# A fused two-layer block on one core: loads moved behind key stores, first key norms on VectorE, wider steps, and four key tasks moved into the attention units

## The chip, the cores and the metric

The kernel runs on one NeuronCore of a Trainium2 chip. The metric is the device time of one execution in microseconds (us); of several executions the median is taken. TensorE (PE) multiplies matrices, VectorE (DVE), ScalarE (ACT) and GpSimd (POOL) work on elements, and SyncE (SP) and POOL issue DMAs. Each engine runs its own instructions strictly in order and waits on semaphores of the others.

## What is computed

x has the shape (4, 512, 512): 4 batches of 512 rows, handled as 16 tiles of 128 rows. Four residual blocks follow each other:

```
x = x + ssm(ctx, layernorm(x))            # state-space scan over ctx
x = x + experts(layernorm(x))             # 64 experts, 8 per row, weighted sum
q = rmsnorm(layernorm(x) @ Wq, gq)        # 16 heads of 128
k = rmsnorm(ctx @ Wk, gk); v = ctx @ Wv
x = x + softmax(q @ k.T / sqrt(128)) @ v @ Wo
x = x + ffn(layernorm(x))                 # weights and activations quantized
```

Everything but the quantized parts is float32.

## The kernel before

The program has three stages: the state-space stage, the expert stage and the attention stage with the feed-forward work. The change lies at the seam of the last two and inside the third.

**Key tasks.** The keys of a batch b and head h are one *key task* (class `Keys`): `task` multiplies Wk of the head with ctx of the batch on PE (two matmuls of 128x512, shown by the profile as four passes, L1231), `evict` squares the result on ACT (L1241), scales it into SBUF as kT (L1243) and stores kT to k_dram through SP (L1246), `squares` sums the squares with four matmuls against ones (L1255), and `take` writes the mean squares with ACT (L1267). The 64 key tasks are placed wherever PE is thought to have room. Nine are done in the expert stage, one after each of the first experts (`key_tasks`, called from `run_in`): heads 6 and 7 of batches 2 and 3, and heads 3 to 7 of batch 1. Sixteen are left for the attention stage (`KEYS_LATE`: heads 8 to 15 of batches 2 and 3): eight among its first steps, eight in its units. The inverse roots of their mean squares are made for all late keys at once in `last_keys`, and stored as rows in r_dram.

**First steps of attention** (`attend`, 1436 to 1530 us of the profile). PE can't start a head before the four row tiles of batch 0 have their expert outputs. For each tile, POOL issues eight gathers from y_dram (`fetch`, L1876; a gather moves 128 rows of 2 KB, 256 KB), DVE adds each to x with its weight (`add`, L1884), and then come the layernorm statistics (`stats`: two DVE operations and two of POOL, ve and rstd), the normalized tile (`normed`, DVE, xn_c), its transpose on PE (`turn_x`, copied by ACT), and for each of two head groups the queries: `queries` (PE pq, ACT squares), `norm_q` (DVE sum, POOL qms and rq), `scale_q` (DVE qn) and `turn_q` (PE pqt, ACT qT). `scores` then starts the first head: PE psc, DVE maximum mx, ACT exponential e; `weights` and `turn` divide and transpose e. Between these stand eight key tasks (`some_keys`) and the loads `load_q` (Wq of a head group, 1 MB) and `load_kv` (kT, its norm row rk broadcast to 128 partitions, and v: 256 KB each). `norm_k` multiplies kT by rk, on POOL (L1944).

The order of all this is written out by `later(time, f)`: a list of steps with nominal times, sorted, and then emitted in that order. So a nominal time fixes only the order in which each engine gets its instructions, not when they run. GAP = 1.25 is the distance of two gathers; FLIGHT = 3.5 the distance of a gather and its add. The gathers of the four tiles follow each other without a break, so the last additions of a tile stand among the first of the next one. Gathers use four buffers in turn; `wide` gives tile 0 four more.

**Units.** From then on the order is by units: unit u = 4n+i handles row tile i of head n; `put(front/back, u, ...)` hangs other work onto units, the eight remaining key tasks among it (units 7, 11, ... 35; sums one unit later), and `last_keys`.

Buffers in the pool `late` are shared by tag: "Th" and "hq" hold the ctx of batches and later feed-forward tiles, "hid" holds Wk of eight heads.

Of the kernel before, what the change touches and what calls it, by code (L numbers as in the profile page):

```python
# [29 lines left out]
P = 128  # L30
# [27 lines left out]
HG = 4  # L58

KEYS_LATE = [(b, h) for b in (2, 3) for h in range(8, H)]  # L60
# [730 lines left out]
def moe_phase(ctx, cm, x_all, w, kv, dr, router_stats, out):  # L791
# [28 lines left out]
    with tc.manual_schedule():  # L820
        attend(cm, x_all, w, kv, y_dram, r["wk"], r["pos"], tern, late, ctx_k, keys.wk, out)
# [380 lines left out]
class Keys:  # L1202
# [14 lines left out]
    def load(self, h0, h1, pool, tag):  # L1217

        t = pool.tile([P, self.KC, (h1 - h0) * HD], F32, name="k_w", tag=tag)
        for h in range(h0, h1, HG):  # L1220
            cols = slice(h * HD, min(h + HG, h1) * HD)
            self.nc.sync.dma_start(t[:, :, cols.start - h0 * HD:cols.stop - h0 * HD],
                                   self.w["Wk"][:, cols].rearrange("(k p) e -> p k e", p=P))
        for h in range(h0, h1):
            self.wk[h] = t[:, :, (h - h0) * HD:(h - h0 + 1) * HD]
# [9 lines left out]
    def evict(self, vec=None):  # L1235

        if self.pk is None:
            return
        b, h, pk = self.pk
        sq, kT = self.row("sq"), self.row("kT")  # L1240
        self.nc.scalar.activation(sq, pk, AF.Square)  # L1241
        if vec is None:
            self.nc.scalar.activation(kT, pk, AF.Copy, scale=self.cm.gkq)  # L1243
        else:
            vec.tensor_scalar(kT, pk, self.cm.gkq, None, ALU.mult)
        self.nc.sync.dma_start(self.kv["k"][b, h], kT)  # L1246
        self.pk, self.sq = None, (b * H + h, sq)
# [11 lines left out]
    def take(self):  # L1259
        if self.pss is None:  # L1260
            return
        i, pss = self.pss
        if self.direct is None:
            ms = self.small.tile([P, self.KB], F32, name="k_ms")
        else:
            ms, self.direct = self.direct[:, 0:self.KB], self.direct[:, self.KB:]
        self.nc.scalar.activation(ms, pss, AF.Copy, bias=EPS, scale=1.0 / HD)  # L1267
        if self.direct is None:
            self.nc.sync.dma_start(self.kv["ms"][:, i * self.KB:(i + 1) * self.KB], ms)
        self.pss = None  # L1270
# [178 lines left out]
def key_tasks(keys, w, pool, late, ps):  # L1449

    nc = keys.nc
    left = [(b, h) for b in (2, 3) for h in (6, 7)] + [(1, h) for h in range(3, H // 2)]
    late_b = KEYS_LATE[0][0]
# [5 lines left out]
    def load(b0, h0, b, h):  # L1459

        if b != b0:
            t = ctx[b] = late.tile([P, CTX // P, S], F32, name="k_ctx",
                                   tag="hq" if b > late_b else "Th")
            nc.sync.dma_start(t, w["ctxT"][:, b * S:(b + 1) * S].rearrange("(k p) s -> p k s",
                                                                           p=P))
        if h // (2 * HG) != h0 // (2 * HG):
            h0 = h // (2 * HG) * 2 * HG
            keys.load(h0, h0 + 2 * HG, late, "hid")

    def task(n):  # L1470
        keys.task(*left[n])
        keys.evict()
        if n + 1 < len(left):
            load(*left[n], *left[n + 1])
        else:
            load(*left[n], late_b, KEYS_LATE[0][1])

    load(-1, -1, *left[0])
# [366 lines left out]
def attend(ctx, cm, x_all, w, kv, y_dram, wk, pos, tern, late, ctx_k, wk_k, out):  # L1845
# [95 lines left out]
    def norm_k(n):  # L1941
        if n < len(heads):
            kT, rk = ks[n]
            nc.gpsimd.tensor_tensor(kT, kT, rk, ALU.mult)  # L1944
# [252 lines left out]
    ms = pool[1].tile([P, n_ms], F32, name="k_ms")  # L2197
    inside = [False]

    def key_row(n):  # L2200

        if not inside[0]:
            return pool[7].tile([P, S], F32, name=f"k_{n}", tag="oT")
        return (late.tile([P, S], F32, name="k_kT", tag="Th") if n == "kT" else
                pool[1].tile([P, S], F32, name="k_sq", tag="xn_d"))

    def key_bank(shape, name):
        if name == "kpss":
# [5 lines left out]
                lambda b: (ctx_k[b], 0), direct=ms)  # L2214
    keys.wk = wk_k
    first = KEYS_LATE[0][1]
    load_q(0)
    load_kv(0)
# [6 lines left out]
    GAP, FLIGHT = 1.25, 3.5  # L2225

    wide = pool[1].tile([P, KB, S], F32, name="yg_first", tag="eT")
    for n in range(NC * TOPK):
        later(n * GAP, fetch, 1, wide[:, n - KB] if KB <= n < 2 * KB else None)
        later(n * GAP + FLIGHT, add, 1)  # L2230
    for i in range(NC):
        end = (i + 1) * TOPK * GAP + FLIGHT
        later(end, stats, i, "c")
        later(end + 2.5, normed, i, "c")
        later(end + 3, turn_x, i)
        for g, t in ((0, end + 4), (1, end + 9)):
            later(t, queries, 0, g, i)
            later(t + 5.5, norm_q, 0, g)
            later(t + 8, scale_q, 0, g)
            later(t + 8.5, turn_q, 0, g, i)  # L2240
        later(end + 14, scores, 0, i)
        if i < KB - 1:
            later(end + 18, weights, 0, i)
        if i < KB - 2:
            later(end + 19, turn, 0, i)
    for f, n, time in ((load_q, 1, 6), (load_kv, 1, 12), (load_kv, 2, 18),
                       (norm_k, 0, 20.5), (norm_k, 1, 30.5), (norm_k, 2, 40.5)):
        later(time, f, n)

# [6 lines left out]
    def last_keys():  # L2256
        rsqrt(nc, small, ms, ms, "late")
# [10 lines left out]
    for i in range(H // 2):  # L2268
        later(2.6 * i if i < 7 else 22, some_keys, *KEYS_LATE[i])
# [9 lines left out]
    for i in range(H // 2):  # L2279
        u = KB * (i + 1) + 3  # L2280
        put(front, u, keys.task, *KEYS_LATE[H // 2 + i])
# [3 lines left out]
    put(back, KB * (H // 2 + 1) + 4, last_keys)  # L2285
# [141 lines left out]
```

## Time and profile before

| what | value |
|---|---|
| median of 3 runs | 2722.08 us (2715.19 to 2722.46) |
| the profiled execution: its time / its span | 2716.06 us / 2714.3 us |
| mean granted PE clock | 0.96 |
| PE busy | 2519.8 us, 93% of the span |
| DVE, ACT, POOL busy | 1519.0, 1234.1, 1175.4 us |
| attention's first PE work / end of the first steps | 1436.5 us / 1529.5 us |

The span is the profiled execution from first to last instruction. "Busy" is the time in which an engine had an instruction in work; "granted clock" is the share of full speed that PE got. The chain of waits follows the work that ended last backwards to what released each step. In a timeline, the number in brackets is how long the engine sat idle before a line, and who released it.

### The profile page before, as it was taken

Reading aid. Unit: us, or ns where it says so; the run is one execution under the profiler, and the core shown is the slowest. Engines: PE = TensorE matmul, PEld = TensorE weight load, DVE = VectorE, ACT = ScalarE, POOL = GpSimd, SP = SyncE. Lnnn points to the kernel's source line nnn. Section 1 sums busy time; section 2 is a strip of 40 time slices with the busy share of each in tenths; the row PEclk is TensorE's granted clock in tenths of the full one; section 3 lists DMA queues with packets and bytes.
Section 4 is the critical chain, followed back from the end, with each engine's and each line's share of the span. In section 5 each row is a group of like instructions: output and inputs, shape, how many; then the busy total and the mean of one; then the engine's idle time right before and its main releaser. Section 6 shows DMA issues by size and latency. Waiting matters only on the chain. (4 is left out here: it accounts for less than half of the span.)

```text
span 2714.3 us, 29922 instructions
## 1 busy us (share of the span) xinstructions
PE 2519.8 (93%) x10151; PEld 1428.1 (53%) x10151; DVE 1519.0 (56%) x2575; ACT 1234.1 (45%) x2351; POOL 1175.4 (43%) x1073
## 2 busy tenths in 40 slices
PE   5989797887899999999998899999999999999997
PEld 2545454554556566666674454445555555555543
DVE  5897989966322244344324555546665666554446
ACT  5666666664323222233322344344555555555543
POOL 3888888960333344444435323223332343211112
PEclk8979798998999999999998899999999999999999
DMA  6253535332656567889866444223332343222100
GB/s 247 90 196 104 199 103 185 117 133 83 203 177 218 187 220 224 284 276 330 279 224 213 125 135 126 87 95 117 128 101 74 120 128 113 70 82 62 56 31 20
DMA packets 199358, 404.67 MB, mean 149 GB/s; under 512 B 30611, under 2 KB 72147, under 8 KB 195104
## 3 DMA queue, kind: packets, MB, share of 16 engines
q1 hardware_dynamic: 156574, 249.33, 27.6%
q0 software_dynamic: 40576, 153.19, 18.0%
q8 instruction: 83, 1.36, 0.2%
q14 instruction: 75, 0.61, 0.1%
q10 hardware_dynamic: 2050, 0.18, 0.1%
HBM read 320.70 MB, written 81.92 MB: 148 GB/s over the span
## 5 line engine op out<-in xcount | busy, mean ns | idle before, releaser
L1989 DVE TENSOR_REDUCE mx<-psc 128x1 f32<-128x512 f32 x256 | 176.8, 691 | 459.0 <-PE psc L1986 459.0
L1335 PE MATMUL pg<-xT,wg 128*128 128x284 f32 (+12 forms) x1536 | 400.9, 405 | 2.1 <-ACT xT L1322 1.1
L1335 PEld LDWEIGHTS pg<-xT,wg 128*128 128x128 f32 x1536 | 283.6, 195 | 86.3 <-issue 38.3
L521 POOL TENSOR_TENSOR dBu<-bb,du 128x1024 f32<-128x1024 f32 x128 | 318.1, 2508 | 21.5 <-DVE dA L546 13.6
L1992 ACT ACTIVATE e<-psc,mx 128x512 f32<-128x512 f32 x256 | 176.0, 688 | 309.7 <-DVE mx L1989 309.4
L1986 PE MATMUL psc<-kT,qT 128*128 128x512 f32 x512 | 267.1, 604 | 1.0 <-ACT qT L1980 1.0
L1276 POOL DMA_INDIRECT xg<-xn_dram,tok x168 | 172.1, 1024 | 215.1 <-PE pt L1319 169.8
L2013 PE MATMUL po<-eT,v 128*128 128x512 f32 x512 | 231.5, 595 | 8.1 <-ACT eT L2007 8.0
L1952 PE MATMUL pq<-Wq,xnT 128*128 128x512 f32 x512 | 235.8, 604 | 0.7 <-DMA k_dram<-k_kT 0.7
L2022 PE MATMUL px<-Wo,oT 128*128 128x512 f32 x512 | 231.9, 597 | 0.0
L532 ACT ACTIVATE dA<-delta,negA 128x512 f32<-128x512 f32 x256 | 176.8, 694 | 86.9 <-DVE hc L547 76.6
L2006 PEld LDWEIGHTS pet<-ident,e 128*128 128x128 f32 x1024 | 127.8, 142 | 146.2 <-issue 119.8
L1963 POOL TENSOR_SCALAR qms<-qms 128x4 f32<-128x4 f32 x64 | 24.8, 388 | 413.2 <-DVE qms L1961 412.4
L546 DVE TENSOR_TENSOR_SCAN dA<-dA,dBu 128x1024 f32<-128x1024 f32 x80 | 184.9, 2311 | 21.1 <-POOL dBu L521 14.6
L552 PE MATMUL yT<-ident,hc 128*128 128x128 f32 x1024 | 143.4, 290 | 41.1 <-POOL hc L547 23.7
L552 PEld LDWEIGHTS yT<-ident,hc 128*128 128x128 f32 x1024 | 127.1, 151 | 100.7 <-issue 56.3
L1380 DVE COPY yo<-po 128x512 f32<-128x512 f32 x68 | 47.0, 691 | 219.2 <-PE po L1369 219.2
L2013 PEld LDWEIGHTS po<-eT,v 128*128 128x128 f32 x512 | 96.3, 190 | 134.3 <-issue 115.9
L1876 POOL DMA_INDIRECT yg<-y_dram,pos x124 | 125.4, 1011 | 87.0 <-issue 62.9
L2006 PE MATMUL pet<-ident,e 128*128 128x128 f32 x1024 | 155.3, 275 | 7.7 <-DVE e L1998 7.7
L2007 ACT COPY eT<-pet 128x512 f32<-128x512 f32 x256 | 148.0, 578 | 6.1 <-PE pet L2006 6.1
L1276 POOL DMA_INDIRECT wd<-down,widx x64 | 63.4, 990 | 200.9 <-PE po L1369 169.0
(356 smaller groups left out, 4442.2 us busy)
## 6 DMA issues: line engine op xcount, KB each, us to landing
y_dram<-yo SPq DMA_DIRECT2D x110, 256.0 KB
bb<-bc_dram SPq DMA_DIRECT2D x16, 1024.0 KB
cb<-bc_dram SPq DMA_DIRECT2D x16, 1024.0 KB
v_dram<-v SPq DMA_DIRECT2D x64, 256.0 KB
k_dram<-k_kT SPq DMA_DIRECT2D x64, 256.0 KB
Wq<-Wq SPq DMA_DIRECT2D x16, 1024.0 KB
kT<-k_dram SPq DMA_DIRECT2D x64, 256.0 KB
rk<-r_dram SPq DMA_DIRECT2D x64, 256.0 KB
```

The lines of the kernel that those rows point to most:

```text
L521: nc.gpsimd.tensor_tensor(dBus[q], st[b]["bb"][i // 2][:, j:j + 2, :], st[b]["du"][c].unsqueeze(1).to_broadcast([P, 2, S]), ALU.mult)
L532: nc.scalar.activation(dAs[q][:, j, :], st[b]["delta"][c], AF.Exp, scale=negA[:, c, n:n + 1])
L546: nc.vector.tensor_tensor_scan(*flat, 0.0, ALU.mult, ALU.add)
L552: nc.tensor.matmul(yT[:, lc, :], t[:, lc * P:(lc + 1) * P], cm.ident, is_transpose=True, start=first and lc == 0, stop=last, skip_group_ch ...
L1276: nc.gpsimd.indirect_dma_start(out=t[0:n, :], out_offset=None, in_=table, in_offset=bass.IndirectOffsetOnAxis(ap=index, axis=0))
L1335: nc.tensor.matmul(pg[:, 0:n], s["wg"][:, c, m * P:(m + 1) * P], s["xT"][:, c, 0:n], start=c == 0, stop=c == NC - 1)
L1952: nc.tensor.matmul(pq.rearrange("p h d -> p (h d)"), xnTs[b * NC + i][:, c, :], s["Wq"][:, c, :], start=c == 0, stop=c == NC - 1)
L1986: nc.tensor.matmul(pscore, st[b, g]["qT"][:, h, i * P:(i + 1) * P], ks[n], start=True, stop=True)
L1989: nc.vector.tensor_reduce(mx, pscore, AX.X, ALU.max, negate=True)
L2006: nc.tensor.transpose(pt[:, kc, :], e[:, kc * P:(kc + 1) * P], cm.ident)
L2013: nc.tensor.matmul(po, v[:, kc, :], eT[:, kc, :], start=kc == 0, stop=kc == KB - 1)
L2022: nc.tensor.matmul(px, oTs[j * HG + h][:, i * P:(i + 1) * P], st[b, g]["Wo"][:, h, :], start=h == 0, stop=h == HG - 1)
```

## The change

- `KEYS_LATE` begins at head 6: heads 6 and 7 of batches 2 and 3 leave the expert stage (five key tasks are left there, and ctx is loaded three times for them rather than four) and go to the units, which now hold twelve key tasks (units 7 to 51); `last_keys` moves from unit 40 to unit 56. Late keys go in the order of heads, batches 2 and 3 in turn; both ctx stay in "Th" and "hq". Wk of heads 6 and 7 is loaded over that of heads 8 and 9 (`load_last`) during the first steps. In the units kT is made and stored in two halves of 256 columns, in the buffers "xq" and "Tx".
- `load_kv(0)` was issued by SP before anything else but Wq; now it comes at nominal time 8.1, behind the stores of the first four key tasks. The other loads move from 6, 12, 18 to 13.3, 17, 25.
- The first three `norm_k` run on VectorE instead of GpSimd.
- Tiles start 12 apart (TILE) instead of 10, FLIGHT is 5 instead of 3.5, `wide` also serves tile 1, and the steps that follow a tile's last add stand 0.5 to 1.7 nearer to it. In the emitted order, each tile's statistics and `normed` now stand on DVE ahead of the next tile's adds; the first head's maximum of tile i-1 (mx) and the second group's query sum (qms) of tile i-1 now stand on DVE ahead of `normed` of tile i, where they stood behind it; and on PE psc of tile i-1 is ahead of the transpose of tile i.

```diff
-KEYS_LATE = [(b, h) for b in (2, 3) for h in range(8, H)]
+KEYS_LATE = [(b, h) for b in (2, 3) for h in range(6, H)]
...
 # evict: parts is one tile, or two halves
+        for n, kT in enumerate(parts):
+            cols = slice(n * S // len(parts), (n + 1) * S // len(parts))
...
+            self.nc.sync.dma_start(self.kv["k"][b, h, :, cols], kT)
...
 # key_tasks
-    left = [(b, h) for b in (2, 3) for h in (6, 7)] + [(1, h) for h in range(3, H // 2)]
+    left = [(1, h) for h in range(3, H // 2)]
...
+        if n + 1 == len(left):
+            load(2, "Th")
+            keys.load(H // 2, H, late, "hid")
+
+    load(1, "Th")
+    keys.load(0, H // 2, late, "hid")
+    load(3, "hq")
...
 # attend
-    def norm_k(n):
+    def norm_k(n, engine=nc.gpsimd):
...
+    order = [(b, h) for h in list(range(8, H)) + [6, 7] for b in (2, 3)]
...
     load_q(0)
-    load_kv(0)
...
-    GAP, FLIGHT = 1.25, 3.5
+    GAP, FLIGHT, TILE = 1.25, 5, 12
...
-    for n in range(NC * TOPK):
-        later(n * GAP, fetch, 1, wide[:, n - KB] if KB <= n < 2 * KB else None)
-        later(n * GAP + FLIGHT, add, 1)
     for i in range(NC):
-        end = (i + 1) * TOPK * GAP + FLIGHT
+        for k in range(TOPK):
+            later(i * TILE + k * GAP, fetch, 1, wide[:, k - KB] if k >= KB and i < 2 else None)
+            later(i * TILE + k * GAP + FLIGHT, add, 1)
+        end = i * TILE + TOPK * GAP + FLIGHT - 0.5
         later(end, stats, i, "c")
-        later(end + 2.5, normed, i, "c")
-        later(end + 3, turn_x, i)
-        for g, t in ((0, end + 4), (1, end + 9)):
+        later(end + 2, normed, i, "c")
+        later(end + 2.6, turn_x, i)
+        for g, t in ((0, end + 3.5), (1, end + 8.5)):
...
-        later(end + 14, scores, 0, i)
+        later(end + 13, scores, 0, i)
...
-    for f, n, time in ((load_q, 1, 6), (load_kv, 1, 12), (load_kv, 2, 18),
-                       (norm_k, 0, 20.5), (norm_k, 1, 30.5), (norm_k, 2, 40.5)):
+    for f, n, time in ((load_kv, 0, 8.1), (load_q, 1, 13.3), (load_kv, 1, 17), (load_kv, 2, 25)):
         later(time, f, n)
+    later(24, load_last)
+    for n in range(3):
+        later(20.5 + 12 * n, norm_k, n, nc.vector)
...
-    for i in range(H // 2):
+    rest = order[H // 2:]
+    for i, (b, h) in enumerate(rest):
         u = KB * (i + 1) + 3
-        put(front, u, keys.task, *KEYS_LATE[H // 2 + i])
+        put(front, u, keys.task, b, h)
...
-    put(back, KB * (H // 2 + 1) + 4, last_keys)
+    put(back, KB * (len(rest) + 1) + 4, last_keys)
```

## The prediction

> **What bounds the kernel now.** I read the page first: PE is busy for 93% of the span and its slices stand at 9 nearly everywhere, so a change pays where PE waits, or where PE work is put into such waits. Next the busy time by stretches, cut at the transposes of the four row tiles (1460.29, 1478.95, 1496.01, 1513.12) and at the second head's first scores (1529.5):
>
> ```profile
> core 0: us, PE busy (x) PEld busy (x) DVE busy (x) ACT busy (x) POOL busy (x), PEclk, DMA share, GB/s
> 1436.50:1460.29 23.79, 20.35 (x76) 11.82 (x77) 9.40 (x14) 8.72 (x20) 12.88 (x14) 0.86 0.97 345
> 1460.29:1478.95 18.66, 15.29 (x44) 8.60 (x45) 10.70 (x14) 3.60 (x7) 14.90 (x17) 0.77 0.73 217
> 1478.95:1496.01 17.06, 12.34 (x35) 5.87 (x36) 10.14 (x17) 5.67 (x10) 11.93 (x13) 0.88 0.31 90
> 1496.01:1513.12 17.11, 13.25 (x34) 6.39 (x35) 10.37 (x15) 3.37 (x7) 10.15 (x12) 0.80 0.28 78
> 1513.12:1529.50 16.38, 11.66 (x38) 5.72 (x37) 5.88 (x10) 5.14 (x11) 4.87 (x8) 0.94 0.53 176
> ```
>
> PE is idle for 20 of these 93 us, and much of what it does runs at a reduced clock (PEclk, third column from the end: 0.77 to 0.88 in the first four). DMA is full only in the first stretch. The chain of waits says what the path is:
>
> ```profile
> 1439.20 7.25 DMA yg<-y_dram,pos
> ...
> 1449.21 7.20 DMA yg<-y_dram,pos
> ...
> 1486.99 3.43 DMA yg<-y_dram,pos
> ...
> 1612.60 3.43 PE po L2013 x8
> ...
> 1631.13 3.43 PE po L2013 x8
> ...
> 1740.17 3.43 PE po L2013 x8
> ...
> 1757.09 3.43 PE po L2013 x8
> ```
>
> Gathers lead the first steps, and the same 256 KB takes 7.2 us from issue to landing early, 3.4 us later. After 1530 the chain is PE alone: a unit group of a head takes 18.53 us with a key task (1612.60 to 1631.13) and 16.92 without (1740.17 to 1757.09; others 16.48). The timeline of the first steps:
>
> ```profile
> 1457.10 0.69 DVE L1890 BATCH_NORM_STATS2 st_c<-x_all 128x6 f32<-128x512 f32 x1
> ...
> 1460.29 1.12 PE L1909 MATMUL pt<-ident,xn_c 128*128 128x128 f32 x4 [3.44 <-DVE xn_c L1902]
> ...
> 1483.17 0.62 POOL L1963 TENSOR_SCALAR qms<-qms 128x4 f32<-128x4 f32 x1 [3.69 <-DVE qms L1961]
> ...
> 1497.81 4.82 PE L1952 MATMUL pq<-Wq,xnT 128*128 128x512 f32 x8
> ...
> 1503.90 2.48 DVE L1884 SCALAR_TENSOR_TENSOR x_all<-yg,wk,x_all 128x512 f32<-128x512 f32 x1
> ...
> 1504.54 1.28 POOL L1944 TENSOR_TENSOR kT<-kT,rk 128x512 f32<-128x512 f32 x1
> ```
>
> Tile 0's statistics begin at 1457.10 because DVE first had to add a gather of tile 1 (landed 1456.4); tile 0's own last add was done at 1455.4. PE waited 3.44 us for it. POOL waited 3.69 us in qms with tile 2's gathers queued behind. An add of 0.75 us took 2.48 us beside POOL's norm of kT. And the expert stage, for the moved key tasks:
>
> ```profile
> 837.58 1.98 PE L1231 MATMUL pk<-k_ctx,k_w 128*128 128x512 f32 x4
> 839.39 1.88 PE L1359 MATMUL po<-wd,h 128*128 128x512 f32 x4
> ...
> 853.63 1.88 PE L1359 MATMUL po<-wd,h 128*128 128x512 f32 x4
> ...
> 857.63 1.05 PE L1255 MATMUL kpss<-ones,k_sq 128*128 128x1 f32 x8
> ...
> 866.03 1.98 PE L1359 MATMUL po<-wd,h 128*128 128x512 f32 x4
> ```
>
> PE has no gap here: an expert takes 14.24 us with a key task (839.39 to 853.63) and 12.40 without its matmuls but still with its sums of 0.92 us, so 11.5 us without either.
>
> **Tile 0.** Ahead of its gathers SP issued Wq (1 MB) and kT, rk, v (768 KB). Now only Wq is ahead. The last gather of tile 0 is issued at 1447.96 as before (POOL's order up to there is the same). With 3.4 to 5 us to land it is there by 1451.4 to 1453, its add is done by 1453.8, statistics take 0.69 + 0.18, ve and rstd 0.64 + 0.58, xn_c 0.54: 1456.4. PE has its six key tasks until 1456.86 and then goes on without a gap: **pt(0) at 1456.9, 3.4 us earlier**, and no more than that, because the key tasks then end last. If the gathers still take 7.2 us, it is 1458.5, since the statistics no longer stand behind tile 1's adds: 1.8 us.
>
> The Trainium skill ("DMA: Bandwidth & Descriptors", section "Queues, rings and completion order") has each DMA engine take turns between the queues it has work for, packet by packet; a gather on POOL's queue would then give up about its own 256 KB to SP's queue, and 768 KB less on that queue would bring it almost nothing. The row speaks against so mild a share: 7.25 us beside the loads, 3.43 without. By the rule alone this term would be the 1.8 us.
>
> **Tiles 1 to 3.** What is late next? In the new order normed of tile i stands on DVE behind mx and the second qms of tile i-1, so the tiles form one ring. From pt to the next pt: pt 0.63, ACT's copy 0.58, pq 3.44 (1519.17 to 1522.61), pqt 0.44 and pet 0.44 of older work, second pq 3.44, pqt 0.63, qT 0.58, psc 1.0, mx 0.69, qms 0.67, xn_c 0.55: 13.1 us. Ten handovers of some 0.08 us (pqt 1523.21, qT 1523.30) add 0.8. The first pq after PE's wait runs slow: 4.42, 4.82 and 4.85 us where 3.60 is the full-speed row, so 1.0 us more. **15 us**, if nothing else is later. The other engines: POOL has 8 gathers at 1.25, ve and rstd 0.8, two times qms and rq at 1.22, and handovers: 14 us, and up to 15.4 where it waits for a qms. DVE has 8 adds at 0.75, the layernorm's 1.4, mx 0.69, two qms and two qn at 0.68, division 0.65 and the norm of kT, which the trace has not on DVE: the nearest row, x_all+px, takes 0.68; 12.2 us in all. It stands behind three adds, by when rk and kT (issued near 1450 behind four stores) have been in flight for over 10 us. On POOL it cost 1.28 us and held up DVE for some 1.7. The ring stays the longest. Between tile 0 and 1 the ring has a key task and a second kpss (1.72 + 2 x 0.81) in place of pqt and pet, but PE doesn't wait in it: 16 us.
>
> So pt(1) at 1472.9 (was 1478.95), pt(2) at 1488, pt(3) at 1503, and the tail of 16.4 us, whose order is nearly the old one, ends at 1519.3 where 1529.5 was: **-10.2 us**. Bounds: rings of 14 us (POOL alone) and the tail 1 us shorter, -14; rings of 17 as now, -3.4 or even -1.8.
>
> The skill ("TensorE: Matmul & The Clock Gate", Part 1) has PE's clock halved only after an idle window of about 3.4 us. The slow pq at 1497.81 followed idle times of 2.95 and 0.78 us with work between, so the row is less kind. By the rule, with gaps of 2 us, the 1.0 us of slow pq per ring would go, and the sum would be 3 us lower.
>
> **Four key tasks moved.** Expert stage: 4 x (14.24 - 11.5) = -11.0 us; experts without key tasks that follow later (912.30, 923.73, 935.16) stand 11.4 us apart with PE full, so nothing else takes over. Units: with key task 18.53, without 16.48 to 16.92, so 1.85 each, **+7.4**; a key task's own PE time is 1.72 + 0.81 = 2.53, the rest falls into short waits. Sum **-3.6**. Bounds: full price in units, +10.1 and so -0.9; or the stall of 1700 to 1712 (PE waits 1.95 us for e, which DVE made in 2.27 us beside POOL's norm) goes with the longer units: that group took 20.4 instead of 16.9 us, so -7.
>
> **At nothing.** The halves of kT: ACT twice about 0.4 instead of 0.69 us and one more store per key task; ACT is busy for 9 of 20 us there (1600 to 1620), SP needs 0.4 us per issue. If ACT's 0.15 to 0.2 us came onto the path, 12 x 0.2 = 2.4 us. `load_last` (256 KB) is due some 90 us before its first reader. The third ctx load at the experts' start (512 KB) has the stage to land; at the first stretch's 345 GB/s it holds others up by at most 1.5 us. `last_keys` moves, its two table loads of 1.28 us and PE's wait of 1.44 us with it.
>
> **Sum:** -10.2 - 3.6 = -13.8 us. The profiled execution took 2716.06 us (span 2714.3); it would take 2702.3. The four known times (2715.19, 2716.06, 2722.08, 2722.46) lie in two pairs, with 2718.9 as their mean; which pair a median falls on I can't tell, so I add the 2.8 us and say **2705**.
>
> **Rivals.**
> - *The wait only moves.* SP now issues Wq of the second group and kT, rk, v of head 1 (1.75 MB) near 1455 to 1459, in front of tile 1's gathers; these take 7.2 us instead of 4. For: the first stretch moved 345 GB/s at a share of 0.97. Against: xn_c(1) has some 1.5 us of slack behind mx. Loss 2 to 4 us once: 2708.
> - *The rings stay at 17.* In-order waits between POOL's rq and DVE's adds cost 2 us per tile as they do now (3.69 us in qms). Then -3.4 - 3.6 = -7, with one ring gained: 2713 with moved tasks nearer -2.
> - *Moved tasks aren't free.* Units pay 10.1 and the expert stage, held by gathers, gives nothing; against it speak PE's rows without gaps. -10.2 + 10.1: 2719.
> - *The ring closes at half clock* (slower). psc of tile i-1 now precedes pt(i) on PE and mx precedes xn_c on DVE, so PE has nothing to do while the chain goes round; if the clock falls in each gap and stays down, both pq cost 3.44 us more and pqt, pet, psc some 2 together: 13.9 + 8.9 = 22.8 us. Three rings 68.4 instead of 52.8 are +15.6, with -3.4 and -3.6: 2727.5. It decides from a ring of 20 us on ((52.8 + 7) / 3).
>
> **Numbers.** Forecast 0.58 (2698 to 2712 as its own range); wait moves 0.11; rings at 17, 0.14; moved tasks dear 0.07; half clock 0.10. A difference under 0.3%, 8 us, can't be told from none here. Faster by more: 0.55 + 0.09 + 0.07 = 0.71; within: 0.03 + 0.02 + 0.07 + 0.07 = 0.19; slower: 0.10. The range runs from 2696 (both terms at their best, 2718.9 - 21, with 2 us for the lower pair of runs) to 2718; it leaves out the slower rival and half of the dear tasks.
>
> **What would show it.** Right: pt(0) near 1457 after the shift of the expert stage by some 11 us (attention's first PE work near 1425.5, so pt(0) near 1446), distances of the transposes of 16, 15, 15 us, gathers of tile 0 landing within 5 us, adds of 0.75 us without the 2.5 us ones, unit groups of 18.5 us for twelve heads. Wrong: distances of 17 or more, with mx or qms as DVE's last wait; attention starting less than 8 us earlier; unit groups above 19 us with ACT named before eT.

## The result, and the profile after

The changed kernel takes 2717.6 us (median of 12 runs), the kernel before 2719.6 (12 runs in turn with them): a ratio of 0.9996 with a 95% interval of 0.9983 to 1.0009, so no difference that could be told. The forecast was 13.8 us less. The profiled execution has a span of 2715.5 us (before: 2714.3).

So the question is where 13.8 us went. Three cuts through the span answer most of it: attention's first PE work, po(0), which is the first multiplication by v and ends the first steps, and po(16), behind all late key tasks. Kernels tried below leave one or two of these stretches as they are, so that each can be read from several profiles: of the table's values for the kernel before, the second ones come from experiment 7 and the 1439.8 from experiment 4; for the changed kernel, the second ones come from experiment 1, and the eleven starts from it and the ten versions that keep its expert stage.

| stretch | before | changed | forecast difference | measured |
|---|---|---|---|---|
| start to attention's first PE work | 1436.5, 1438.5, 1439.8 | eleven profiles, 1423.3 to 1431.8, mean 1427.5 | -11.0 | -10.7 (of means) |
| first PE work to po(0) | 99.5, 99.9 | 94.8, 97.8 | -10.2 | -3.4 |
| of this, to xn_c of tile 0 | 23.2, 23.0 | 19.4, 18.7 | -3.4 (as pt) | -4.0 |
| po(0) to po(16) | 270.8, 270.8 | 281.3 | +7.4 | +10.6 |
| po(16) to po(63) | 835.3, 839.0 | 839.8 | 0 | the same work: 835.3 to 839.8 in all profiles |

The sum of the means is -3.5 us, inside the timed interval (-4.6 to +2.4). Two terms came as forecast, the expert stage and tile 0; two did not: the rings of tiles 1 to 3 (a ring is the way from one tile's transpose pt to the next tile's) with the tail behind them, and the units. The busy time by stretches of the changed kernel, cut at the transposes pt of the four tiles and at the second head's first psc, as it was shown for the kernel before:

```profile
core 0: us, PE busy (x) PEld busy (x) DVE busy (x) ACT busy (x) POOL busy (x), PEclk, DMA share, GB/s
1427.34:1447.56 20.22, 20.22 (x76) 11.76 (x77) 7.75 (x12) 8.03 (x19) 11.46 (x13) 0.86 0.85 271
1447.56:1466.19 18.63, 14.50 (x48) 7.41 (x47) 10.02 (x17) 6.41 (x14) 11.51 (x14) 0.91 0.95 335
1466.19:1481.63 15.44, 11.95 (x34) 5.59 (x35) 11.75 (x20) 4.11 (x8) 12.82 (x15) 0.86 0.48 136
1481.63:1498.14 16.51, 12.97 (x34) 6.01 (x35) 11.44 (x19) 4.11 (x8) 10.16 (x13) 0.81 0.35 97
1498.14:1516.61 18.47, 13.50 (x35) 6.69 (x35) 4.60 (x8) 3.52 (x7) 4.68 (x7) 0.78 0.47 156
```

Read the second column, the lengths, against the forecast 16, 15, 15 and 16.4: they are 18.63, 15.44, 16.51, 18.47, 6.65 us more in sum, and with 69.05 nearly what the kernel before needed (69.21). In tile 0 PE has no gap any more (20.22 of 20.22). The high DMA share (next to last column) has moved from the first stretch into the second: 0.97 and 0.73 before, 0.85 and 0.95 now. And the last two rows have the lowest PE clock. PE's timeline shows where:

```profile
1456.68 5.40 PE L1949 MATMUL pq<-Wq,xnT 128*128 128x512 f32 x8 [1.58 <-DMA Wq<-Wq]
...
1466.19 0.66 PE L1906 MATMUL pt<-ident,xn_c 128*128 128x128 f32 x4 [1.83 <-DVE xn_c L1899]
1467.52 5.23 PE L1949 MATMUL pq<-Wq,xnT 128*128 128x512 f32 x8 [0.67 <-ACT xnT L1908]
1473.46 3.60 PE L1949 MATMUL pq<-Wq,xnT 128*128 128x512 f32 x8
...
1481.63 1.08 PE L1906 MATMUL pt<-ident,xn_c 128*128 128x128 f32 x4 [1.92 <-DVE xn_c L1899]
1483.39 5.82 PE L1949 MATMUL pq<-Wq,xnT 128*128 128x512 f32 x8 [0.67 <-ACT xnT L1908]
...
1499.91 6.10 PE L1949 MATMUL pq<-Wq,xnT 128*128 128x512 f32 x8 [0.68 <-ACT xnT L1908]
```

In each ring PE waits 1.8 to 1.9 us for xn_c, and the pq behind the wait takes 5.2 to 6.1 us where 3.60 is full speed and 4.6 was forecast. VectorE's timeline says what xn_c waits for, and, in tile 1, what the adds wait for:

```profile
1455.17 0.75 DVE L1881 SCALAR_TENSOR_TENSOR x_all<-yg,wk,x_all 128x512 f32<-128x512 f32 x1 [4.91 <-DMA yg<-y_dram,pos]
...
1478.72 0.18 DVE L1889 BATCH_NORM_AGGREGATE mv_c<-st_c 128x2 f32<-128x6 f32 x1
1479.75 0.69 DVE L1986 TENSOR_REDUCE mx<-psc 128x1 f32<-128x512 f32 x1 [0.84 <-PE psc L1983]
1480.36 0.68 DVE L1958 TENSOR_REDUCE qms<-sq 128x4 f32<-128x512 f32 x1
1480.95 0.54 DVE L1899 TENSOR_SCALAR xn_c<-x_all,mv_c,rstd_c 128x512 f32<-128x512 f32 x1
```

Tile 2 has its statistics at 1478.90 and rstd (POOL) at 1479.89, but xn_c stands behind mx and qms of tile 1 and begins at 1480.95. In the units, what the forecast lacks is in one place:

```profile
1729.76 3.60 PE L2010 MATMUL po<-eT,v 128*128 128x512 f32 x8
...
1745.36 0.41 PE L2272 MATMUL pkr<-ident,k_ms 128*80 128x128 f32 x1 [4.10 <-DVE k_ms L100]
1745.56 1.92 PE L1983 MATMUL psc<-kT,qT 128*128 128x512 f32 x2
...
1748.12 4.80 PE L1949 MATMUL pq<-Wq,xnT 128*128 128x512 f32 x8
...
1753.61 3.60 PE L2010 MATMUL po<-eT,v 128*128 128x512 f32 x8
```

The group from po(12) to po(13), which has `last_keys`, takes 23.85 us (1729.76 to 1753.61); without it 16.92, as the next group and both neighbours in the kernel before. The wait of 4.10 us is more than half of the difference; behind it psc takes 1.92 us and pq 4.80, where 1.02 and 3.60 are full speed. In the kernel before `last_keys` cost 1.7 us (the group from po(8) to po(9) took 18.20 instead of 16.5). ScalarE shows why:

```profile
1738.81 0.60 ACT L1977 COPY qT<-pqt 128x512 f32<-128x512 f32 x1
1741.30 0.59 ACT L1908 COPY xnT<-pt 128x512 f32<-128x512 f32 x1 [1.88 <-PE pt L1906]
1741.90 1.28 ACT L95 ACT_TABLE_LOAD   x1
1743.19 0.27 ACT L95 ACTIVATE rs_t_late<-k_ms 128x80 f32<-128x80 f32 x1
```

Unit 56 also turns a tile of x. That transpose stands on PE behind px (1737.22 to 1740.66), its copy on ScalarE ahead of the table load, so the load, the root, five operations of VectorE and PE's wait of 4.10 us begin only when PE is out of work. At unit 40 in the kernel before the load ran beside px, at 1677.25, and PE waited 1.44:

```profile
1675.50 3.60 PE L2022 MATMUL px<-Wo,oT 128*128 128x512 f32 x8
...
1677.25 1.28 ACT L95 ACT_TABLE_LOAD   x1
...
1680.54 0.27 PE L2259 MATMUL pkr<-ident,k_ms 128*64 128x128 f32 x1 [1.44 <-DVE k_ms L100]
```

**Theory:** (1) `last_keys` is dear because of its place; (2) mx and qms ahead of xn_c make PE wait, and the wait costs twice, by itself and by the clock of the next pq; (3) the DMA engines are full until tile 1 is turned, so what tile 0 gains by earlier gathers tile 1 loses. **Rivals:** `last_keys` is dear by its size; the rings are closed by the gathers on GpSimd (8 of 1.3 us and two norms of 1.9, about 15 us per tile); the moved key tasks, or the load and halves that come with them, are the loss.

### The profile page after: what moved, and what is told of

Read it like the earlier page. It is cut to its first block, busy times and chain, and to the rows that moved or that the text cites. A ratio compares the mean times of both kernels' runs of the same rounds, so it can differ in the third digit from the quotient of the medians.

```text
span 2715.5 us, 29937 instructions
## 1 busy us (share of the span) xinstructions
PE 2520.7 (93%) x10151; PEld 1425.0 (52%) x10151; DVE 1518.0 (56%) x2578; ACT 1236.5 (46%) x2363; POOL 1172.2 (43%) x1070
## 5 line engine op out<-in xcount | busy, mean ns | idle before, releaser
L521 POOL TENSOR_TENSOR dBu<-bb,du 128x1024 f32<-128x1024 f32 x128 | 318.3, 2510 | 21.3 <-DVE dA L546 13.5
L546 DVE TENSOR_TENSOR_SCAN dA<-dA,dBu 128x1024 f32<-128x1024 f32 x80 | 184.9, 2311 | 20.3 <-POOL dBu L521 14.7
L552 PE MATMUL yT<-ident,hc 128*128 128x128 f32 x1024 | 141.2, 287 | 41.0 <-POOL hc L547 21.9
L1949 PEld LDWEIGHTS pq<-Wq,xnT 128*128 128x128 f32 x512 | 95.8, 197 | 103.0 <-issue 98.3
```

Source lines behind the costliest of these rows:

```text
L521: nc.gpsimd.tensor_tensor(dBus[q], st[b]["bb"][i // 2][:, j:j + 2, :], st[b]["du"][c].unsqueeze(1).to_broadcast([P, 2, S]), ALU.mult)
L546: nc.vector.tensor_tensor_scan(*flat, 0.0, ALU.mult, ALU.add)
L552: nc.tensor.matmul(yT[:, lc, :], t[:, lc * P:(lc + 1) * P], cm.ident, is_transpose=True, start=first and lc == 0, stop=last, skip_group_ch ...
L1949: nc.tensor.matmul(pq.rearrange("p h d -> p (h d)"), xnTs[b * NC + i][:, c, :], s["Wq"][:, c, :], start=c == 0, stop=c == NC - 1)
```

## Experiments

All are made from the changed kernel unless said otherwise. "Distances" are those of pt from tile 0 to 1, 1 to 2 and 2 to 3, and "the start" is attention's first PE work; po(0) is also given counted from it, since the expert stage ends at a different time in each profile. Spans are those of one profiled execution.

**1. `last_keys` at unit 64**

```diff
-    put(back, KB * (len(rest) + 1) + 4, last_keys)
+    put(back, KB * (len(rest) + 1) + 12, last_keys)
```

> The changed kernel (span 2715.5) with last_keys moved from unit 56 to unit 64, where no tile of x is turned. Theory: what it costs is its place. At unit 56 ScalarE first has xnT of turn_x to copy, which waits for PE behind a px, so its table load starts 4 us late and PE waits 4.10 us for the norms. At unit 64 PE's wait for k_ms is about 1.4 us again (as in the kernel before), the group of units from po(12) to po(13) goes from 23.85 to about 17 us, the one that has it now, po(14) to po(15), grows by about 1.7, and the span is some 5 us shorter, 2710. Rival: the operation itself has become dear, by its four more heads: the group that has it grows by 6 to 7 us wherever it stands, and the span stays at 2715.

Measured: po(12) to po(13) 16.9, po(14) to po(15) 18.4 (16.5 without), po(0) to po(16) 276.3 instead of 281.3, span 2710.6. ScalarE and PE:

```profile
1774.80 1.28 ACT L95 ACT_TABLE_LOAD   x1
```

```profile
1773.05 3.60 PE L2019 MATMUL px<-Wo,oT 128*128 128x512 f32 x8
1778.26 0.28 PE L2272 MATMUL pkr<-ident,k_ms 128*80 128x128 f32 x1 [1.61 <-DVE k_ms L100]
```

The table load runs beside px again, PE waits 1.61. It is the place, not the size: 5.0 us. The first steps, which this edit doesn't touch, took 97.8 us here and 94.8 in the changed kernel's own profile: their spread is at least 3 us, and no single pair of profiles settles less than that. The units are steadier: po(0) to po(16) took 276.3 us in all four versions with `last_keys` at unit 64.

**2. The first head's scores behind the next tile's turn**

```diff
-        later(end + 2, normed, i, "c")
+        later(end + 1.4, normed, i, "c")
...
-        later(end + 13, scores, 0, i)
+        later(end + 15.2, scores, 0, i)
```

> The changed kernel with the first head's scores of a tile (psc, mx) set behind the next tile's turn: on VectorE xn_c now stands ahead of mx and qms, on PE pt ahead of psc. In the changed kernel the distances of pt from tile to tile are 18.6, 15.4, 16.5 us, and the second head's first psc is 18.5 after the last pt. Theory: xn_c is late because mx and qms stand ahead of it. Then xn_c follows rstd at once, 1.0 us earlier in each of tiles 1 to 3, and PE's wait before pt falls from 1.9 to about 0.9; po(0) comes at about 1519 instead of 1522.2, and if the shorter wait leaves PE at its full clock (pq 3.6 instead of 5.2 to 6.1) at about 1514. Rival: the gathers set the ring (GpSimd issues eight of them, 1.3 us each, and two norms of 1.9 us per tile, about 15 us): the distances stay within 0.3 us of 15.4 and 16.5 and po(0) at 1522.

Measured: distances 17.0, 15.6, 15.0; po(0) 90.6 after the start (94.1 to 98.2 in seven profiles with the scores at their place), span 2708.4. VectorE, tile 3:

```profile
1490.91 0.75 DVE L1881 SCALAR_TENSOR_TENSOR x_all<-yg,wk,x_all 128x512 f32<-128x512 f32 x1 [0.68 <-DMA yg<-y_dram,pos]
...
1493.92 0.18 DVE L1889 BATCH_NORM_AGGREGATE mv_c<-st_c 128x2 f32<-128x6 f32 x1
1495.12 0.55 DVE L1899 TENSOR_SCALAR xn_c<-x_all,mv_c,rstd_c 128x512 f32<-128x512 f32 x1 [1.02 <-POOL rstd_c L1893]
```

Now xn_c follows rstd at once and the adds wait for gathers: theory and rival are both right, one after the other. mx and qms cost 1.5 to 2.2 us in the last distance (16.5 to 17.2 in the seven others); below that the gathers close the ring near 15, the rival's figure (experiments 9 and 10 have one ring each of 14.3). The surest part lies behind the rings: from pt(3) to po(0) it is 22.0 us, where the seven have 24.0 to 24.2. PE's wait was expected to fall and did not; it rose from 1.9 to 2.8, since psc now stands behind pt, and pq stayed slow (5.0).

**3. Loads later in the program**

```diff
-    for f, n, time in ((load_kv, 0, 8.1), (load_q, 1, 13.3), (load_kv, 1, 17), (load_kv, 2, 25)):
+    for f, n, time in ((load_kv, 0, 8.1), (load_q, 1, 13.3), (load_kv, 1, 36), (load_kv, 2, 46)):
...
-    later(24, load_last)
-    for n in range(3):
-        later(20.5 + 12 * n, norm_k, n, nc.vector)
+    later(41, load_last)
+    for n, time in enumerate((20.5, 46.5, 58.5)):
+        later(time, norm_k, n, nc.vector)
```

> The changed kernel with the loads of kT, rk and v for heads 1 and 2 and of the two last heads' Wk moved from tile 1 (times 17, 25, 24) to tiles 2 and 3 (36, 46, 41), and the norms of keys 1 and 2 behind them (46.5, 58.5). Theory: tile 1's gathers and Wq of the second group land late because 2 MB of these loads share the DMA engines with them. Then VectorE's wait of 4.91 us for a gather of tile 1 falls under 2.5, PE's wait of 1.58 for Wq goes, the distance of pt from tile 0 to 1 falls from 18.6 to 16 and po(0) comes 2.5 us earlier, at about 1519.7; tiles 2 and 3 keep 15.4 and 16.5, since the DMA engines are lightly loaded there. Rival 1: the gathers take that long by themselves or behind Wq alone: the distance stays above 18. Rival 2: the loads then slow the gathers of tiles 2 and 3: their distances grow by 1 us or more each and po(0) stays.

Measured: distances 18.6, 16.4, 16.7, po(0) 98.2 after the start: no gain, rival 1. But the loads had moved less than was meant:

```profile
1455.40 0.44 SPq L1929 DMA_DIRECT2D kT<-k_dram  x1
```

That is kT of head 1, 30.8 us after the start instead of 21.3 (1448.59 in the changed kernel); that of head 2 went out at 33.1 instead of 29.1, still ahead of tile 1's last add (35.4), since nothing on SP's queue behind the last store of keys has to wait. PE's wait for Wq was gone (pq at 1454.38 without a wait), and the distance did not shrink.

**4. The four tasks stay with the experts** (the changed first steps alone; `key_tasks` and `KEYS_LATE` as before)

```diff
-KEYS_LATE = [(b, h) for b in (2, 3) for h in range(6, H)]
+KEYS_LATE = [(b, h) for b in (2, 3) for h in range(8, H)]
...
-    order = [(b, h) for h in list(range(8, H)) + [6, 7] for b in (2, 3)]
+    order = [(b, h) for b in (2, 3) for h in range(8, H)]
...
-    later(24, load_last)
```

> The changed first steps alone: the four key tasks stay with the experts, as in the kernel before (span 2714.3), eight tasks in units, last_keys at unit 40, no late load of Wk. Theory: the move of the four tasks is a loss (9.3 us gained with the experts, 10.6 lost in the units), the first steps a gain of 4.6 us. Then attention starts at 1436.5 as before, po(0) comes 4.6 us before that of the kernel before, at 1531.4, and the span is 2709.7. Rival 1: the late load of Wk (0.5 MB) and the halves of kT are what holds the first steps up: they gain 6 to 10 us here, and the span is 2704 to 2708. Rival 2: the move carries the gain, and the first steps lose as soon as the stores of key tasks are not fewer: span 2714 or more.

Measured: attention starts at 1439.8 (3.3 us later than in the first profile of the kernel before), distances 16.0, 15.3, 16.8, po(0) 94.1 after the start, units to po(16) 269.1, span 2714.1. The first steps gain 5.6 us here, between the theory's 4.6 and rival 1's 6 (its load of Wk is 256 KB in the profile); one profile can't decide between them. That the move was a loss is not confirmed: with means of several profiles the expert stage gives 10.7, the units take 10.6, of which 5.2 are `last_keys`: as it stands, the move gains nothing.

**5. One Wq** (group 1's queries are made with group 0's Wq, so their values differ; 1 MB less is loaded)

```diff
+    st[0, 1] = {"Wq": st[0, 0]["Wq"]}
...
-    for f, n, time in ((load_kv, 0, 8.1), (load_q, 1, 13.3), (load_kv, 1, 17), (load_kv, 2, 25)):
+    for f, n, time in ((load_kv, 0, 8.1), (load_kv, 1, 17), (load_kv, 2, 25)):
```

> The changed kernel without the 1 MB load of Wq for the second group of heads: that group's queries are made with the first group's Wq, so their values differ. In three profiles of these first steps the distance of pt from tile 0 to tile 1 was 18.1 to 18.6 us, and the DMA engines were full for the whole of 1447 to 1462 (share 1.04 to 1.06, 370 to 400 GB/s). Theory: the engines' capacity holds tile 1 up, and the wait for gathers has only moved there from tile 0, where the kernel before has it (share 1.02 to 1.06 from 1446 to 1461). 1 MB less at 390 GB/s is 2.7 us: the distance falls to about 16, the time at full share to about 12 us, and VectorE's waits for gathers between pt(0) and pt(1), 6.4 to 7.5 us in sum, to under 4.5. Rival: a gather behind others of its own queue takes 7 to 8 us with or without Wq: the distance stays above 17.5.

Measured: distances 17.1, 18.8, 17.2; VectorE's waits for gathers behind pt(0) 6.5 us in sum, as before; po(0) 97.7 after the start. Theory (3) is not borne out in its size: 1 MB less gave 1 to 1.8 us of the 2.7 (17.1 against 18.1 to 18.9 with Wq), and that came back one tile later (18.8). The next loads on SP's queue (Wq of group 2 and Wo), no longer waiting for a Wq buffer, went out at 1458 and 1459, which fits; it was not tested by itself.

**6. Both mends, 1 and 2 together**

> The changed kernel with both edits that gained alone: last_keys at unit 64 (12 to 13 took 16.9 instead of 23.8, 14 to 15 18.4 instead of 16.5: 5.0 us) and the first head's scores behind the next tile's turn (po(0) 4.4 to 6 us earlier). Theory: they touch different stages and add up: span 2715.5 less 9 to 11, about 2705, 0.35 % faster than the kernel before, interval below 1. Rival: what the first steps gain is lost in the later units, where waits for stores vary by 2 to 4 us: 2709 or more, not to be told from the kernel before.

Measured: 2704.7 us, 0.9952 of the kernel before (0.9936 to 0.9969); span 2702.9, po(0) 86.4 after the start, units to po(16) 276.3. They add up. This version is 0.5% faster than the kernel before; the changed kernel's interval against the same kernel (0.9983 to 1.0009) lies wholly above, so it beats that one too. The first steps are those of experiment 2 and took 4.2 us less than there (90.6): the spread again.

**7. The kernel before once more**

> The kernel before once more, for the spread of its profile. If the stages are steady, attention starts within 1 us of 1436.5, the distances of pt are 18.7, 17.1, 17.1 within 0.5 and po(0) comes 99.5 after the start. If what was read from one pair of profiles is partly chance, start and length differ by 2 us or more, as they did for the changed kernel's first steps (95.0 and 97.8 us with the same steps) and for the experts with the four tasks (1436.5 and 1439.8).

Measured: start 1438.5, distances 17.4, 17.1, 16.2, po(0) 99.9 after the start, span 2720.2. The length of the first steps is the same in both profiles of the kernel before (though pt(0) came 26.3 us after the start instead of 23.8); start and later units are not: po(16) to po(63) took 839.0 instead of 835.3.

**8. The first norms back on GpSimd**

```diff
-        later(20.5 + 12 * n, norm_k, n, nc.vector)
+        later(20.5 + 12 * n, norm_k, n)
```

> The changed kernel with the first three keys' norms back on GpSimd, at the same places. Theory: each norm then stands for some 1.5 us between GpSimd's gathers, which are what the ring closes by in tiles 2 and 3, and an add beside it takes 2.5 us instead of 0.75 as in the kernel before: the distances of tiles 1 to 2 and 2 to 3 grow by 1 to 2 us each, po(0) by 2 to 4 us. Rival: the ring is closed by PE and VectorE (pt, pq, qms, mx, xn_c) and GpSimd has slack: distances and po(0) stay within 1 us.

Measured: distances 18.9, 17.2, 16.9, po(0) 97.7 after the start, against 94.8 and 97.8 with the norms on VectorE. The adds of 2.3 us are back:

```profile
1473.94 2.30 DVE L1881 SCALAR_TENSOR_TENSOR x_all<-yg,wk,x_all 128x512 f32<-128x512 f32 x1 [0.84 <-DMA yg<-y_dram,pos]
```

The mechanism is there, a loss of 2 to 4 us isn't shown: the difference is 0 to 3 us, as large as the spread.

**9. PE kept at work** (two matmuls more, of which nobody reads the result, ahead of pt of tiles 1 to 3)

```diff
+    def fill():
+        t = pav.tile([P, S], F32, name="fill", tag="po")
+        for _ in range(2):
+            nc.tensor.matmul(t, cm.ident, st[0, 0]["Wq"][:, 0, :], start=True, stop=True)
...
+            later(end + 13.2, fill)
```

> The changed kernel with two matmuls more before the turn of tiles 1 to 3 (128x512, 0.9 us each, into a spare accumulator that nobody reads), so that PE works through most of its wait of 1.8 to 1.9 us for xn_c. Theory: the first pq of a tile runs at half clock (5.2 to 6.7 us in tiles 2 and 3 of the changed kernel's profiles) because PE stood still before it; with PE at work it takes 3.7, and the way from the last pt to po(0) falls from 24.0 to 24.2 to about 21.7. The distances of tiles 1 to 2 and 2 to 3 fall by 1 us at most, then the gathers close the ring at 15. Rival: the wait before pt isn't what halves the clock (with one Wq less, a pq behind the same waits of 1.83 and 0.68 took 3.70): pq stays above 5 and the way at 24.

Measured: distances 18.7, 17.0, 14.2; from pt(3) to po(0) 21.9 us instead of 24.0 to 24.2; po(0) 92.5 after the start, span 2712.3. PE, tiles 2 and 3:

```profile
1481.73 3.11 PE L1995 MATMUL fill<-Wq,ident 128*128 128x512 f32 x4
1484.68 0.60 PE L1906 MATMUL pt<-ident,xn_c 128*128 128x128 f32 x4
1485.95 3.70 PE L1949 MATMUL pq<-Wq,xnT 128*128 128x512 f32 x8 [0.68 <-ACT xnT L1908]
...
1496.85 1.88 PE L1995 MATMUL fill<-Wq,ident 128*128 128x512 f32 x4
1498.93 0.63 PE L1906 MATMUL pt<-ident,xn_c 128*128 128x128 f32 x4 [0.20 <-DVE xn_c L1899]
1500.23 3.70 PE L1949 MATMUL pq<-Wq,xnT 128*128 128x512 f32 x8 [0.68 <-ACT xnT L1908]
```

pq takes 3.70 in all three tiles, behind the same 0.68 us for xnT. So the slow pq comes with the wait before pt, and more work shortens the way to po(0) by 2.2 us, as expected, with one ring of 14.2 (14.25). Where the fill itself ran slow (3.11, xn_c was done at 1483.7), it pushed pt back and took its gain away. That the whole kernel gets faster is not shown: this version was timed once.

**10. Both mends and three such matmuls**

> The version with both mends (last_keys at unit 64, the first head's scores behind the next tile's turn; span 2702.9) with three such matmuls more before the turn of tiles 1 to 3, where PE waits 2.7 us. Theory: the clock stays up, pq takes 3.7 in each tile (it took 3.68, 4.45, 3.76 there, and 4.94, 4.56, 5.01 with the one mend alone); the gathers close the ring at 15.0, so the distances stay and only the tail gains: 0 to 3 us, span 2700 to 2703. Rival: the matmuls push pt back where xn_c comes before they are done, 0.5 to 1 us per tile, and nothing is gained: 2703 to 2706.

Measured: 2706.1 us, 0.9948 of the kernel before (0.9928 to 0.9968), span 2703.9; pq 3.68 in all three tiles, from pt(3) to po(0) 17.5 us, distances 18.3, 14.3, 16.8 (the last with a fill of 4.44 us). Not to be told from the mends alone.

**11. Loads held back** (heads 1 and 2 and the late Wk are loaded from ScalarE's queue, behind the turn of tile 1)

```diff
-    def load_kv(n):
+    def load_kv(n, queue=nc.sync):
...
-    for f, n, time in ((load_kv, 0, 8.1), (load_q, 1, 13.3), (load_kv, 1, 17), (load_kv, 2, 25)):
+    for f, n, time in ((load_kv, 0, 8.1), (load_q, 1, 13.3)):
...
+    for n, time in ((1, 34), (2, 46)):
+        later(time, load_kv, n, nc.scalar)
+    later(41, load_last)
-    later(24, load_last)
-    for n in range(3):
-        later(20.5 + 12 * n, norm_k, n, nc.vector)
+    for n, time in enumerate((20.5, 46.5, 58.5)):
+        later(time, norm_k, n, nc.vector)
```

> The changed kernel with the loads of kT, rk and v for heads 1 and 2 and of the late Wk issued by ScalarE, behind the turn of tile 1, and the norms of keys 1 and 2 later (46.5, 58.5). Where they stood on SP's queue they went out at once, since nothing holds that queue up, so moving them in the program did little; here 2 MB stay out of the DMA engines until tile 1 is turned. In four profiles of the changed first steps it was 38.9 to 41.0 us from the start of attention to pt(1). Theory: the engines' capacity sets that time: 2 MB at 390 GB/s are 5 us, of which about half lies in front of tile 1's last gather, so pt(1) comes at 36.5 to 37.5 and the time at a DMA share above 1 is under 10 us. Rival: the gathers are slow behind the stores of keys and Wq alone: pt(1) stays at 39 or later. If the loads only press on the next tile, the distance of tile 1 to 2 grows over 17 as it did with one Wq less (18.8).

Measured: distances 15.2, 15.6, 16.6, no wait for a gather behind pt(0); but pt(0) came only 26.6 us after the start, pt(1) 41.8, po(0) 98.0.

```profile
1449.95:1465.14 15.19, 12.64 (x48) 6.74 (x47) 6.72 (x12) 6.25 (x13) 7.49 (x9) 1.00 0.53 177
1465.14:1480.75 15.61, 12.07 (x35) 5.59 (x35) 11.13 (x19) 4.11 (x8) 12.08 (x13) 0.87 0.61 171
```

Tile 1's stretch now has a DMA share of 0.53 instead of 0.95, and the short distance. It was not tile 0's gathers that were late: xn_c of tile 0 began 18.5 us after the start, but pt(0) stood on PE behind the sixth and seventh key task, and these had waited (1.18 and 1.45 us) and run slowly (pk 2.64 and 3.76 us instead of 1.96). So the short distance may be that of a late tile 0.

**12. Both mends and the loads held back**

> Both mends together with the loads held back behind the turn of tile 1. With the loads held, tile 0 to 1 took 15.2 us instead of 18.1 to 18.9, and VectorE waited for no gather behind pt(0); with both mends alone it took 13.9 and 18.3 in two versions, the shorter where tile 0 was late. Theory: from the start of attention to po(0) it takes 84 to 87 us (86.4 and 87.6 with the mends alone, 95 to 98 in the changed kernel), the distance of tile 0 to 1 stays under 16, and the span is 2699 to 2703, 0.5 to 0.6 % faster than the kernel before. Rival: the engines' capacity up to pt(1) is shared by stores of keys that PE waits for as well, so what the gathers gain shows up as a later pt(0), and the sum from the start to pt(1) stays at 37 to 41 and the span at 2703 to 2706.

Measured: 2709.6 us, 0.997 of the kernel before (0.9956 to 0.9985), span 2708.4; distances 17.1, 18.0, 17.1, waits for gathers behind pt(0) again 5.8 us, and po(0) 93.5 after the start. The theory is refuted: the held loads don't free tile 1. In the next two rings PE waited 4.6 us for xn_c (2.7 with the mends alone), VectorE 1.9 us for the last gather of each; that fits the held loads landing there, which was not tested by itself. Holding the loads adds nothing to the mends: 2709.6 us against 2704.7, with intervals (0.9956 to 0.9985, 0.9936 to 0.9969) that overlap.

## Why the prediction was wrong, point by point

- **"4 x (14.24 - 11.5) = -11.0 us"** for the expert stage: right, -10.7.
- **Tile 0, "3.4 us earlier"**: right. xn_c comes 18.5 to 20.3 us after attention's start in all versions of the changed steps, 23.0 and 23.2 before; PE goes on without a gap in the changed kernel (20.22 of 20.22 us). The last gather took 5.23 us, just over the 3.4 to 5 us used.
- **"Tiles 1 to 3 ... 15 us" and "the tail of 16.4 us, whose order is nearly the old one"**: the step that failed most, 6.65 us in sum. Its mechanism, the ring through mx and qms, was right (experiment 2), and 15.44 in one ring came as forecast. From pq to psc the path was another one, though, as the chain of waits of the changed kernel has it for the ring of 16.51:

```profile
1483.39 5.84 PE pq L1949 x8
...
1489.88 0.70 DVE qms L1958
...
1491.37 1.56 POOL rq L1961
...
1495.10 1.14 PE psc L1983 x2
```

The forecast went over PE's second pq there; the chain goes over the norm of the queries, with POOL's rq, which the forecast had counted as POOL's work but not in the ring. It is hardly longer (PE waited 0.27 us for qn behind the second pq), so it did not decide. Two terms were too small. The slow pq was entered at 1.0 us per ring and at nothing in the tail; it measured 1.6 and 2.2 in the rings and 2.5 in the tail (5.23, 5.82, 6.10 less 3.60), and taking it out gave 2.2 in the tail (experiment 9). The tail follows a ring in which PE now waits, so the clock at its start was not that of the old order. And the rival "the wait only moves", a loss of 2 to 4 us given 0.11, came true in size: 18.63 instead of 16. What sets it is not settled. In the changed kernel's profile two ways end together:

```profile
1445.80 0.24 POOL L1891 TENSOR_SCALAR ve_c<-mv_c 128x1 f32<-128x1 f32 x1 [3.16 <-DVE mv_c L1889]
...
1446.89 1.08 POOL L1873 DMA_INDIRECT yg<-y_dram,pos  x1 [0.18 <-issue]
...
1461.56 0.74 DVE L1881 SCALAR_TENSOR_TENSOR x_all<-yg_first,wk,x_all 128x512 f32<-128x512 f32 x1
...
1464.40 0.69 DVE L1986 TENSOR_REDUCE mx<-psc 128x1 f32<-128x512 f32 x1 [1.15 <-PE psc L1983]
```

POOL had issued two gathers of tile 1 and then stood in tile 0's ve; the third went out at 1446.89 and was added 8.28 us later (1455.17, above), the last was added at 1461.56, and rstd was done at 1464.41. By the other way mx began at 1464.40, behind psc and a pq that had waited 1.58 us for Wq and then run 5.40; xn_c stood behind it. In all versions of the changed steps the third gather goes out 18.7 to 20.4 us after the start, and from issue to add it takes 8.28 us here, 4.2 to 8.2 in the others; for the fifth gather it is 6.9 to 8.5 us in all but experiment 11 (5.2). That is mostly the rival's 7.2 us and not the 4 us of the forecast. Taking away Wq gave 1 to 1.8 of the 2.7 us that the engines' capacity would give (experiment 5), holding the other loads back gave a short distance once (11) and not again (12). In all versions pt(1) came 36.6 to 41.8 us after the start (forecast 36.4), with a short distance mostly where pt(0) was late. What fills the engines there beyond the gathers (the stores of the key tasks were never taken out) stays open.
- **"The rings stay at 17"**, the rival given 0.14: its size came (the first steps gained 3.4, and the rings of the seven profiles with the scores at their place average 16.9 us). Its cause, waits between POOL's rq and VectorE's adds, was not tested by itself; experiments 2 and 9 show the order of mx and qms and the slow pq at work instead.
- **"Units: ... 1.85 each, +7.4"**: four groups grew by 2.04, 2.05, 2.64 and 2.05 us over their length without a key task (16.5, 16.48, 16.92, 16.92), 8.8 in sum and between the 1.85 and the full price of 2.53; the 2.64 holds 0.23 us of PE's waiting for ACT's first half of kT, a term put at nothing. Against that, the stall that the forecast had only as a bound went away. In the kernel before PE waited 1.95 us there, and the group took 20.37 us instead of 16.92:

```profile
1710.86 0.63 PE L2006 MATMUL pet<-ident,e 128*128 128x128 f32 x4 [1.95 <-DVE e L1998]
```

Less these 3.45 us, the four groups cost 5.3. The rival "moved tasks aren't free" had the size of the units' loss (10.1 against 10.6), but half of it is `last_keys`, and the expert stage gave its 10.7. About half of the stall went without the moved tasks too (the group took 18.67 in experiment 4), so it is partly luck of the alignment.
- **"`last_keys` moves, its two table loads of 1.28 us and PE's wait of 1.44 us with it", at nothing**: wrong. Its price went from 1.7 to 6.9 us. Of a step that is moved I had counted its instructions but not looked at what stands ahead of it on its engine at the new place: turn_x at unit 56. The cover, px, was the same; the copy of xnT used it up.
- **The half clock rival** ended elsewhere: rings of 22.8 us didn't come, since the second pq of tiles 1 to 3 always ran at full speed (3.60). It was priced as all or nothing; it is one pq per wait.
- **"Adds of 0.75 us without the 2.5 us ones"**: right, and worth at most 3 us (experiment 8).
- **The two rules weighed.** The forecast took the gathers' landing time from the rows and not from the rule of turns between queues; with 5.23 us the rows were nearer. For the clock, the Trainium skill ("TensorE: Matmul & The Clock Gate", Part 1) asks for an idle window of about 3.4 us, and says the window is free-running. No wait in these rings exceeds 2 us, and the clock fell all the same, so the sum "3 lower" that this rule would have given was the worse one. That the window runs free agrees with one pair: waits of 1.83 and 0.67 us left pq at 5.23 in the changed kernel, 1.83 and 0.68 left it at 3.70 with one Wq less.

In sum: -13.8 forecast, +6.8 for the first steps (rings and tail), +3.2 for the units with `last_keys` and +0.3 for the experts make -3.5, and -2.0 was timed. The two profiles themselves differ by +1.2, mostly by the spread of the later units, which fell against the changed kernel there (839.8 to 835.3).

## What to carry to other kernels

Before a step with a table load or another long chain is moved, read what stands ahead of it on its engine at the new place, and whether the cover it had is used by that. In a ring of engines with order fixed by hand, look which instructions of the older tile stand ahead of the one that the next tile waits for; and price a PE wait with the slow matmuls behind it, which here cost as much again (1.6 to 2.5 us behind waits of 1.8 to 1.9). Ask of each transfer that is freed earlier whether the engines that carry it have room then: where the share in the stage before was near 1, the wait can turn up again in the next, as it did here (0.97 and 0.73 became 0.85 and 0.95).

## What the runs showed of the hardware that was not expected

- Two useless matmuls in a wait of 1.9 us made the following pq 1.5 to 3.0 us shorter: 3.70 in three of three, instead of 5.2 to 6.7 in 20 of the 21 rings without them (seven profiles with the scores at their place).
- The same code has a spread that is larger than the terms argued about: attention's start lies anywhere from 1423.3 to 1431.8, and the same first steps took 94.8 and 97.8 us, those with the scores behind the turn 90.6 and 86.4.
- In the units DVE's xn_d waits for the store of y (`out<-y`). At one place, near 2250 us (the same code in all fourteen profiles), this wait falls into groups, whatever the kernel: 2.4 to 2.8 us in six, with 35.8 to 36.3 us from po(40) to po(42); 4.04 to 4.29 in six, with 37.5 to 37.7; 4.34 and 4.69 in two, with 39.9 and 40.3, where PE runs dry (1.93 us in the changed kernel) and the next po takes 5.40 us instead of 3.60. The changed kernel's own profile has 4.34, the one of before 2.67: 3.8 us of the difference between them, and no part of the change, for the kernel before has 4.12 in its second profile.
